# A two-layer graph attention network: the order in which the node tiles are walked

## The chip, the core and the metric

The kernel runs on one core of a Trainium2 chip. The core has five engines that run side by side: TensorE (PE in the profile, with its weight loads as PEld), VectorE (DVE), ScalarE (ACT), GpSimd (POOL) and SyncE (SP). POOL issues the indirect DMAs (gathers and scatters by a list of rows), SP most of the plain ones. Sixteen DMA engines move the data. The metric is the device time of one execution in microseconds, as the median of several runs.

## The reference, cut to what matters

There are 10,000 nodes with 768 numbers each, and 170,000 directed edges `src -> dst`, sorted by `dst`, among them a loop at every node. To these the network adds one more loop a node. Two graph attention layers follow, the first with 4 heads of 256, the second with one head of 768. Everything is in float32.

```python
def gat_conv(x, edge_index, W, a_src, a_dst, bias, heads, out_ch, concat):
    xl = (x @ W).reshape(n, heads, out_ch)
    alpha_src = jnp.einsum('nhc,hc->nh', xl, a_src)
    alpha_dst = jnp.einsum('nhc,hc->nh', xl, a_dst)
    e = jax.nn.leaky_relu(alpha_src[src] + alpha_dst[dst], 0.2)
    m = jax.ops.segment_max(e, dst, num_segments=n)
    e = jnp.exp(e - m[dst])
    s = jax.ops.segment_sum(e, dst, num_segments=n)
    alpha = e / (s[dst] + 1e-16)
    out = jax.ops.segment_sum(xl[src] * alpha[:, :, None], dst, num_segments=n)
    ...
h = relu(layer_norm(gat_conv(x, ..., W1, ...))) + (x @ Wr1 + br1)
h1 = h
h = layer_norm(gat_conv(h, ..., W2, ...)) + (h1 @ Wr2 + br2)
return _layernorm(x + h)
```

For each node the rows of its in-neighbours are weighted by a softmax over its in-edges and added up. How much work a node makes depends on its in-degree.

## The kernel before, in words

**Preparation.** While PE computes `x @ W1` for all nodes and writes the products with their attention terms to a table in DRAM (`table1`, rows of 1033 numbers), the other engines sort the nodes by in-degree, from many to few, and write for each node the list of its in-neighbours. The sorted nodes are cut into 79 tiles of 128. `slot_counts` gives each tile a number of slots, the most in-edges that a node in it may have: tile 0 has 41 slots, tiles 1 to 5 have 27, 26, 25, 24 and 24, then the number falls slowly to 20 at tile 16, 16 at tiles 44 to 50, 15 at 51 to 58, 14 at 59 to 64, 13 at 65 to 69, 12 at 70 to 72, 11 at 73 to 75, and 10, 9 and 8 at tiles 76, 77 and 78. There are 1377 slots in all. Slot k of a tile holds, for each of the 128 nodes, the row number of its k-th in-neighbour.

**The order.** `TURNS` (line 96) is the order in which both layers walk the tiles. Before, it takes every other tile from 78 down to 0 and then the others from 1 up to 77. `FIRST` (line 98) gives each tile the place of its first slot in this order. Lines 663 to 666 bring both lists into the order of `TURNS`, so that inside the layers `t` counts turns and `SLOTS[t]` is the count of the tile whose turn it is. If any node doesn't fit its tile's slots, a general path is taken instead; it isn't taken here.

**The ring.** Both layers read the table rows through a `Ring` (line 434): a buffer in SBUF of 28 rows of 128 partitions in layer 1 and 38 in layer 2. The slots follow each other in it in the order of `TURNS`, across tiles. Each gather (line 418, issued by POOL) brings one slot, that is one row for each of the 128 nodes. The gather for slot q + size is written behind the weighted sum that frees slot q. In layer 2 a tile's first slot holds the tile's own rows, which lie together in the table and come by a plain DMA of SP (line 445).

**Layer 1** (`ordered_layer1`, lines 668 to 812). In a turn, the logits of all slots of the tile are computed and turned into weights (`weights_of`, `logits`, `normalised`); this needs all of the tile's rows. The first one to four slots (`on_pe`) are summed on PE by diagonal matrices, the others on DVE (`weigh`, lines 504 and 508), three of four after ACT has scaled the row (`multiply`, line 497). The sum is normalised on DVE (lines 563 to 566), and the residual product is added (line 765). Its transposes go through PE, ACT copies them (line 575), SP stores them (line 777), and PE multiplies them by `W2`; ACT copies the product, and SP stores it as the tile's rows of `table2` (line 730). The normalising and products of a tile stand in the turn of the next one. The weights of the next tile are made during the present one where its slots and a lead of 3 fit the ring (line 795); tiles with more than 25 slots don't, and the one with 41 goes through `attend_parts` in parts.

**Layer 2** (`ordered_layer2`, lines 814 to 946) begins when all of `table2` is stored. Per tile there are the gathers of its slots but the first, a fetch of the tile's rows of `x` (an indirect DMA of POOL) and of the stored transposes (SP), the residual product on PE (`residual`), and weights as before. DVE sums the first 512 columns (`weigh`), PE the other 256 by diagonal matrices (lines 859 and 860). `norms` normalises twice in the turn of the next tile (line 884 adds the residual), and POOL scatters the result rows to the output (line 893).

Of the kernel before, what the change touches and what calls it, by code (L numbers as in the profile page):

```python
# [78 lines left out]
def gnn_kernel(ctx, tc, x, x_cols, src, dst, src_col, dst_col, W1, a_src1, a_dst1, b1, g1, be1, Wr1, br1,  # L79
# [9 lines left out]
    NT = -(-N // P)  # L89
# [3 lines left out]
    CAPS = slot_counts(N, n_edges)  # L93
    SLOTS = CAPS

    TURNS = list(range(NT - 1, -1, -2))
    TURNS += sorted(set(range(NT)) - set(TURNS))
    FIRST, TOTAL = [0] * NT, 0
    for t in TURNS:
        FIRST[t], TOTAL = TOTAL, TOTAL + SLOTS[t]  # L100
# [389 lines left out]
    def doubled(e, t):  # L490
        nc.vector.tensor_scalar(e[:, 0], e[:, 0], loops[:, TURNS[t]:TURNS[t] + 1], None, op0=OP.mult)

# [169 lines left out]

    SLOTS, FIRST = [SLOTS[t] for t in TURNS], [FIRST[t] for t in TURNS]

    def nodes(t):
        return order[:, TURNS[t]:TURNS[t] + 1]

    def ordered_layer1():
        nonlocal ps_big
        with tc.tile_pool(name="b1", bufs=1) as pool, tc.tile_pool(name="small1", bufs=2) as small, \  # L670
# [53 lines left out]
            def store(t):  # L724
# [4 lines left out]
                full = None  # L729
                nc.sync.dma_start(table2[TURNS[t] * P:(TURNS[t] + 1) * P, :], row)  # L730

# [485 lines left out]
```

## Time and profile before

| what | value |
| --- | --- |
| median of 3 runs | 5479.6 us (5479.25 to 5485.96) |
| profiled execution, own time | 5488.77 us |
| its span, first to last instruction | 5487.0 us |
| mean granted clock of TensorE | 0.938 |
| first and last store of `table2` (layer 1) | 975.0 and 3483.8 us |
| first gather of layer 2 | 3487.9 us |
| last gather, last scatter issued | 5425.8 and 5477.2 us |
| gathers, both layers | 2675, 969 ns each on POOL |
| DMA | 1581.74 MB, 288 GB/s over the span |

Times in the profile are counted from the first instruction. A busy share over the whole span mixes three stages: the preparation with the first product (to about 900 us), layer 1 and layer 2. In a timeline, "[0.30 <-issue]" after an instruction says how long its engine was idle before it and what ended that. The granted clock is the share of TensorE's clock pulses that were let through. The chain of work that ended last has only the last scatter in it here, so the order of work was read from the timelines.

### The profile page before, as it was taken

The numbers are of one execution on the slowest core, as the hardware profiler recorded it, in microseconds if no ns is written. First come the engines' busy times: TensorE is split into PE (matmuls) and PEld (weight loads), VectorE is DVE, ScalarE is ACT, GpSimd is POOL, SyncE is SP. The second block draws the span as 40 slices with busy tenths as digits, with TensorE's granted clock in tenths as the row PEclk, the third lists the DMA queues.
The fourth block names the chain that finished last, engine by engine and source line by source line (L and its number), as shares of the span: only waits on it lengthen the run. The fifth ranks groups of instructions, "written<-read, shape, count | busy, mean of one in ns | idle before, by whom it ended". The sixth has DMA issues, their size and how long they took to land. (4 is left out here: it accounts for less than half of the span.)

```text
span 5487.0 us, 58297 instructions
## 1 busy us (share of the span) xinstructions
PE 4754.0 (87%) x15032; PEld 2827.1 (52%) x15032; DVE 4328.8 (79%) x7766; ACT 3148.0 (57%) x8255; POOL 3247.4 (59%) x3238
## 2 busy tenths in 40 slices
PE   8999997999999875478999999799988746888998
PEld 3444443555555543245555555466655524555665
DVE  5784244899998888788999999498877786778998
ACT  3433344788888877678888888244433312333444
POOL 2445455455566555455665554377777775777774
PEclk9999998999999988789999999899998877899999
DMA  4333625899999988789999997699999987999996
GB/s 152 124 95 82 94 91 202 316 328 339 339 361 347 344 303 301 285 315 345 353 359 347 341 329 263 239 340 360 345 333 321 336 297 258 331 323 349 349 355 240
DMA packets 457866, 1581.74 MB, mean 288 GB/s; under 512 B 111851, under 2 KB 116011, under 8 KB 457526
## 3 DMA queue, kind: packets, MB, share of 16 engines
q0 software_dynamic: 328704, 1339.21, 68.3%
q1 hardware_dynamic: 126768, 235.29, 13.1%
q10 hardware_dynamic: 2054, 3.42, 0.2%
q8 instruction: 126, 2.06, 0.2%
q14 instruction: 214, 1.75, 0.1%
HBM read 1431.80 MB, written 146.23 MB: 288 GB/s over the span
## 5 line engine op out<-in xcount | busy, mean ns | idle before, releaser
L418 POOL DMA_INDIRECT ring<-table,slots x2675 | 2591.7, 969 | 1635.6 <-DVE acc L508 402.4
L508 DVE SCALAR_TENSOR_TENSOR acc<-ring,e,acc 128x256 f32<-128x256 f32 (+1 forms) x2538 | 1572.0, 619 | 127.5 <-PE acc L709 52.0
L497 ACT ACTIVATE ring<-ring,e 128x256 f32<-128x256 f32 x3320 | 1351.0, 505 | 0.0
L504 DVE TENSOR_TENSOR acc<-acc,ring 128x1024 f32<-128x1024 f32 x830 | 1022.5, 1232 | 72.8 <-ACT ring L497 1.2
L874 PE MATMUL big<-wr,w 128*128 128x512 f32 (+1 forms) x2528 | 857.9, 493 | 0.0
L169 PE MATMUL big<-w,xT 128*128 128x512 f32 x1896 | 827.7, 598 | 28.9 <-DMA w<-in_W_dram 11.2
L169 PE MATMUL big<-wr,xT 128*128 128x512 f32 x1896 | 834.1, 596 | 0.7 <-ACT xT L575 0.7
L169 PE MATMUL big<-w,hT 128*128 128x512 f32 (+1 forms) x2528 | 832.1, 486 | 1.2 <-ACT hT L575 1.2
L860 PE MATMUL big<-ring,diagonals 128*128 128x256 f32 x2672 | 660.8, 409 | 185.3 <-ACT diagonals L859 177.0
L860 PEld LDWEIGHTS big<-ring,diagonals 128*128 128x128 f32 x2672 | 543.6, 206 | 299.4 <-ACT diagonals L859 201.2
L169 PEld LDWEIGHTS big<-w,hT 128*128 128x128 f32 x2528 | 478.4, 189 | 375.0 <-issue 341.3
L709 PE MATMUL acc<-ring,diagonals 128*128 128x256 f32 x1816 | 456.6, 409 | 247.9 <-ACT diagonals L703 216.5
L874 PEld LDWEIGHTS big<-wr,w 128*128 128x128 f32 x2528 | 488.1, 193 | 350.3 <-issue 317.7
L169 PEld LDWEIGHTS big<-w,xT 128*128 128x128 f32 x1896 | 362.7, 192 | 491.9 <-issue 472.8
L169 PEld LDWEIGHTS big<-wr,xT 128*128 128x128 f32 x1896 | 356.9, 192 | 421.2 <-issue 420.3
L709 PEld LDWEIGHTS acc<-ring,diagonals 128*128 128x128 f32 x1816 | 370.1, 206 | 326.8 <-ACT diagonals L703 235.7
L859 ACT ACTIVATE diagonals<-ident,e 128x128 f32<-128x128 f32 x1336 | 399.6, 387 | 155.6 <-DVE e L488 117.9
L554 ACT ACTIVATE sd<-mv,eps 128x1 f32<-128x1 f32 x237 | 69.8, 294 | 614.0 <-DVE mv L552 613.6
L650 DVE TENSOR_TENSOR scr<-big,as_b 128x1024 f32<-128x1024 f32 x79 | 96.8, 1225 | 391.9 <-ACT row L647 391.9
L655 POOL TENSOR_TENSOR row<-row,none 128x1024 f32<-128x1024 f32 x79 | 187.2, 2369 | 280.5 <-ACT row L647 279.9
L703 ACT ACTIVATE diagonals<-ident,e 128x128 f32<-128x128 f32 x908 | 278.5, 387 | 96.4 <-DVE e L488 96.4
L475 ACT ACT_TABLE_LOAD x153 | 196.3, 1283 | 233.1 <-DVE e L474 205.9
(172 smaller groups left out, 3895.5 us busy)
## 6 DMA issues: line engine op xcount, KB each, us to landing
ring<-table,slots POOLq DMA_INDIRECT x2675, 6.5
table<-row SPq DMA_DIRECT2D x79, 516.0 KB, 3.6
h_d<-hT SPq DMA_DIRECT2D x79, 512.0 KB, 7.2
w<-h_d SPq DMA_DIRECT2D x79, 512.0 KB, 8.4
table<-row SPq DMA_DIRECT2D x79, 385.0 KB, 6.2
ring<-table SPq DMA_DIRECT2D x79, 385.0 KB, 6.5
xT<-in_x_cols_dram SPq DMA_DIRECT2D x79, 384.0 KB, 4.5
wr<-in_Wr_dram SPq DMA_DIRECT2D x2, 3072.0 KB
```

The costliest lines, as they stand in the source:

```text
L169: nc.tensor.matmul(p[:, c:e], aT[:, j, :], w[:, j, c:e], start=(j == 0), stop=(j == k - 1))
L418: nc.gpsimd.indirect_dma_start(out=to, out_offset=None, in_=table, in_offset=bass.IndirectOffsetOnAxis(ap=index, axis=0), **more)
L475: nc.scalar.activation(e, e, AF.Exp)
L497: nc.scalar.activation(row[:, s], row[:, s], AF.Copy, scale=e[:, h:h + 1])
L504: nc.vector.tensor_add(acc[:, :c], acc[:, :c], row[:, :c])
L508: nc.vector.scalar_tensor_tensor(acc[:, s], row[:, s], e[:, h:h + 1], (acc if first is None else first)[:, s], op0=OP.mult, op1=OP.add)
L655: nc.gpsimd.tensor_add(row[:, :C1], row[:, :C1], b1_b)
L703: nc.scalar.activation(diagonals[:, k * H1 + i, :], ident, AF.Copy, scale=e[:, k, i:i + 1])
L709: nc.tensor.matmul(acc[:, c:d], diagonals[:, k * H1 + i, :], ring.slot(FIRST[t] + k)[:, c:d], start=(k == 0 and c % BANK == 0), stop=(k == ...
L859: nc.scalar.activation(diagonals[:, k % G, :], ident, AF.Copy, scale=e[:, k, :])
L860: nc.tensor.matmul(to, diagonals[:, k % G, :], ring.slot(FIRST[t] + k)[:, ON_PE2:C2], start=False, stop=(k == n - 1), skip_group_check=True)
L874: nc.tensor.matmul(r[:, c:d], hT[:, j, :], wr2[:, j, c:d], start=False, stop=(j == K1 - 1 and (d < C2 or not whole(t))), skip_group_check= ...
```

## The change

The order `TURNS` is made differently, and nothing else. After the change it takes all tiles from 78 down to 48 one by one, then every other tile from 47 down to 1, and then the others, 0, 2, 4 and so on, up to 46. `FIRST`, the slots' places in the ring and the order in both layers follow from it. In slots, the order before is 8, 10, 11, 12, 12, 13, ... 24, 26, 41, 27, 25, ... 11, 11, 9; after it is 8, 9, 10, 11, 11, 11, 12, ... 25, 27, 41, 26, 24, ... 17, 16, 16.

```diff
     CAPS = slot_counts(N, n_edges)
     SLOTS = CAPS
 
-    TURNS = list(range(NT - 1, -1, -2))
+
+    TURNS = list(range(NT - 1, NT * 3 // 5, -1)) + list(range(NT * 3 // 5, -1, -2))
     TURNS += sorted(set(range(NT)) - set(TURNS))
     FIRST, TOTAL = [0] * NT, 0
     for t in TURNS:
         FIRST[t], TOTAL = TOTAL, TOTAL + SLOTS[t]
```

## The prediction

> **What bounds the kernel now.** I read the page first, then the stretches by engine, then the order of events on single queues. A tile is 128 nodes of similar in-degree; its "slots" are the rows that it gathers from the table. Tile 0 has 41 slots, tile 77 has 9 and tile 78 has 8. The page's costliest groups say which work grows with slots: gathers on POOL, and the weighted sums on DVE.
>
> ```profile
> PE 4754.0 (87%) x15032; PEld 2827.1 (52%) x15032; DVE 4328.8 (79%) x7766; ACT 3148.0 (57%) x8255; POOL 3247.4 (59%) x3238
> ...
> L418 POOL DMA_INDIRECT ring<-table,slots x2675 | 2591.7, 969 | 1635.6 <-DVE acc L508 402.4
> L508 DVE SCALAR_TENSOR_TENSOR acc<-ring,e,acc 128x256 f32<-128x256 f32 (+1 forms) x2538 | 1572.0, 619 | 127.5 <-PE acc L709 52.0
> ```
>
> No engine is full over the span, so I cut the span at tile boundaries and asked for busy times by stretch. The stretches are: layer 1 with 10 to 13 slots going up, with 15 and 16 slots going up, around the largest tile, the last small tiles; then layer 2 with 11 and 12 slots going up, with 16 slots going up, with 16 slots coming down, and its end. Columns: length, busy time of PE, its weight load, DVE, ACT and POOL, granted clock, DMA share, GB/s.
>
> ```profile
> 975.00:1100.70 125.70, 120.67 (x392) 67.94 (x391) 112.66 (x180) 102.25 (x241) 62.10 (x66) 1.00 0.88 303
> 1323.60:1408.80 85.20, 82.18 (x281) 49.32 (x280) 78.19 (x126) 71.37 (x177) 48.47 (x51) 1.00 0.94 346
> 2105.00:2339.20 234.20, 121.92 (x377) 73.18 (x376) 192.38 (x296) 159.59 (x406) 117.51 (x124) 0.75 0.83 291
> 3392.80:3468.20 75.40, 71.50 (x230) 39.64 (x229) 60.72 (x93) 49.08 (x115) 3.76 (x4) 1.00 0.31 114
> 3546.70:3613.40 66.70, 66.70 (x238) 44.17 (x237) 61.52 (x137) 29.59 (x70) 44.76 (x47) 1.00 0.91 306
> 3811.50:3877.40 65.90, 61.08 (x223) 41.08 (x222) 57.17 (x122) 27.83 (x67) 50.02 (x52) 1.00 0.97 352
> 5136.90:5200.10 63.20, 59.16 (x207) 38.82 (x206) 57.84 (x122) 27.55 (x66) 48.11 (x50) 0.97 0.97 358
> 5430.80:5487.00 56.20, 38.91 (x140) 25.78 (x139) 42.68 (x91) 16.07 (x35) 3.98 (x4) 0.89 0.15 54
> ```
>
> The reader is to see that layer 1's small tiles fill PE (120.67 of 125.70 us) while POOL is half idle, and that layer 1 closes with almost no gathers left (3.76 us of POOL in 75.40). In layer 2's middle POOL is busy 50.02 of 65.90 us, which looks like slack. The timeline of POOL shows that it isn't:
>
> ```profile
> 3564.86 0.97 POOL L418 DMA_INDIRECT ring<-table,slots  x1 [0.30 <-issue]
> 3569.03 0.94 POOL L418 DMA_INDIRECT ring<-table,slots  x1 [3.19 <-PE big L860]
> 3570.28 0.94 POOL L418 DMA_INDIRECT ring<-table,slots  x1 [0.30 <-DVE acc L508]
> ...
> 5424.52 0.94 POOL L418 DMA_INDIRECT ring<-table,slots  x1 [0.30 <-issue]
> 5425.77 1.11 POOL L418 DMA_INDIRECT ring<-table,slots  x1 [0.30 <-issue]
> ...
> 5441.03 1.02 POOL L893 DMA_INDIRECT out_dram<-out,order  x1 [10.30 <-ACT out L891]
> ```
>
> Every gather is followed by 0.30 us in which nothing can run, so 1.25 us is the least distance between two. In the stretch 5000 to 5425 no wait is above 0.3 us: the queue is full. Adding all gaps above 0.31 us from the first normalised tile (3546.7) to 5430.8 gives 85.6 us, 57 of them by the end of tile 0; 9.3 us lie in the first seven small tiles, where the ring of 38 rows is full and PE is slower than POOL (the 3.19 above). So layer 2 is the POOL queue: 1298 gathers, 79 residual fetches and 79 scatters.
>
> In layer 1 I use the stores of finished rows, one a tile:
>
> ```profile
> 1000.13 0.32 SPq L730 DMA_DIRECT2D table<-row  x1
> 1025.27 0.32 SPq L730 DMA_DIRECT2D table<-row  x1
> ...
> 3443.10 0.32 SPq L730 DMA_DIRECT2D table<-row  x1
> 3468.23 0.33 SPq L730 DMA_DIRECT2D table<-row  x1
> ...
> 3483.77 0.32 SPq L730 DMA_DIRECT2D table<-row  x1
> ```
>
>
> Up to 13 slots the stores come every 25.1 us, up and down alike; the last takes 15.5. Read the same way, 14 slots take 26.9 going up and 26.3 coming down, 15 and 16 take 28.3 (DVE has no idle there), 18 take 30.3, 20 about 35 up and 34 down. These are costs of a tile, not of its place.
>
> **The change part by part.** It permutes tiles; in layer 1 two tiles fewer straddle the ring's end (46 for 48), which saves two additions of 0.20 us on DVE and two copies on ACT, and nothing else is added or removed. A moved tile takes all of its work along: in layer 1 its gathers and x fetch on POOL, its two stores on SP, its sums, products and copies; in layer 2 one gather fewer (its own rows come through SP), the fetch, the scatter, and SP's load of h. The list preparation copies the same columns to other offsets, beside the layer-0 products: nothing. The fifteen odd tiles 49 to 77 (200 slots) move from each layer's end to its front half, between their neighbours; 2 to 46 and 1 to 47 swap sides. Both layers still open with tile 78; both now close on tile 46 with 16 slots.
>
> *Layer 1, start.* The second tile has 9 slots, not 10. DVE waited 0.57 us at 937.5 for that tile's last rows; one gather less removes it: −0.6.
>
> *Layer 1, small tiles.* Eight tiles of 9 to 12 slots follow on each other going up, at PE's 25.1: 201. Before, four of them took 101.0 going up (starts of the line that adds the residual, L765, 948.5 to 1049.5) and 71, 73 and 75 took 72.5 at the end, where DVE ran ahead of PE; tile 77 stood last and is counted next. 201 less 25.1 for tile 77 is 176, against 173.5: +2.5. Three tiles of 14 slots pay 26.9 instead of 26.3 to 26.5: +1.2.
>
> *Layer 1, end.* Tile 77's 25.1 comes into the row and a tile of 28.3 goes out of it: −3.2. Closing then costs, from L765 of tile 44: 1.1, then 13 rows on DVE at 20.0 (tile 47's own row of sums, 3042.88 to 3065.60, less 2.7 for the next tile's logits, of which there is none), 4.4 of normalising; then 18.1 to the last store, which is today's 23.2 without the 5.1 that the finished row waited for PE. Sum 43.7; today 3441.4 to 3483.8 is 42.4: +1.3. Layer 1 in all: +1.2.
>
> *The largest tiles.* Before, 26 → 41 → 27 come in the order 24, 26, 41, 27, 25; after, 25, 27, 41, 26, 24. A tile gets its weights ahead only if its slots + 3 fit the ring of 28, so three tiles per layer still go without (27, 41, 26). I take 0. Bounds: the unprepared 26 took 42.1 going up, the 27 took 52.6 coming down; half of that 10 either way, ±5 a layer.
>
> *Layer 2, POOL's count.* From its first gather (3487.9) to its last (5425.8) POOL issues 1449 of 1456; seven come behind, two fetches and five scatters. With 38 rows of ring and 16 slots a tile, the last gather goes out at row 10 of tile 42: all fetches are gone by then (that of tile 46 at row 8), and so is the scatter of tile 40: three scatters stay behind. Four more ahead of the last gather, each (1937.9 − 91.6 idle) / 1449 = 1.274: +5.1. The 91.6 is 85.6 and some 6 of DMA waits at the start.
>
> *Layer 2, going up.* With a full ring a tile takes what PE needs: 15.5 for 10 slots, 16.0 for 11, 17.6 for 12, 18.0 for 13 (distances of L884); 9 slots, by the slope of the first two, 15.1. POOL needs slots + 1 instructions of 1.274. The difference is lost: 2.4, 1.5, 0.7, 1.0 and 0.2. Over all fourteen it is 10.1, over the six of them that went up before 4.7: +5.4. Bounds: 0, if POOL's own slower instructions fill it, and +11, if the measured 9.3 of seven tiles counts in full for twice as many.
>
> *Layer 2, end.* Today 61.2 us pass from the last gather to the end (5487.0). After, POOL is the bound until its last gather, and the state is that of tile 47 coming down: its last gather at 5156.2, L884 of the tile two before it at 5158.9, 2.7 later. Then tile 44 at its own work, 19.6 (PE and DVE have 59.16 and 57.84 us for three such); tile 46 without a successor's product, like tile 77's 10.7 plus seven rows of 0.76 = 16.0; then today's 14.1. Sum 52.4: −8.8. Bounds: −1.9, if it keeps the steady lag of 45.2 from last gather to L884 (45.2 + 14.1 = 59.3), and −12.
>
> Layer 2: 5.1 + 5.4 − 8.8 = +1.7. Both layers: **+2.9 us**. The profiled execution took 5488.8 (span 5487.0 and 1.8 around it), 0.17% above the median 5479.6; 5488.8 + 2.9 = 5491.7 on its scale, and on the median's **5482.5**.
>
> A rule that speaks against the new end: in the stretch of 16 slots coming down the granted clock is 0.97, around the largest tile 0.75, because PE waits for rows there; among the small tiles it is 1.00. The Trainium skill, "TensorE: Matmul & The Clock Gate", section "HAM oscillation — how this bites in real kernels", says that a pause of PE over some 3.4 us puts its clock to half. By the rule two such pauses at layer 2's new end would cost about 1.7 us each, an estimate from that page: 5486 instead of 5482.5. I stay with the rows, since the 19.6 already is a stretch with that clock.
>
> **The rivals.**
> (a) *POOL runs dry on the long climb of layer 2 (slower).* Thirty tiles with small steps come first, and what POOL loses behind a full ring is not caught up. The first seven tiles lose 1.33 us each. If all 29 between tile 78 and tile 48 lose that, it is 38.6 instead of 9.3: +29 in place of +5.4, so 5506. It decides from about 0.8 us a tile (23 us, so +14 in place of +5.4, and +11 in all). For it: 14 slots pace 18.5 on PE, close to POOL's 19.1. Against it: from tile 62 on the loss is 0.0.
> (b) *Gathers bound layer 1 as well, and shorter ends are kept (faster).* From the last gather of a tile to its L765 pass 62.9 us at tile 77, 53.3 at tile 47: −9.6. With −8.8 in layer 2, +5.1, and nothing lost on the climb: −13.3, 5466. Against it: POOL in layer 1 waits for DVE and PE in each tile (62.10 busy of 125.70).
> (c) *The order at the peak matters*: if an unprepared 27 on the way up costs what it cost coming down, and the 26 gains nothing, +10.5 in layer 1 and +13.2 in layer 2 (37.4 against 24.2): 5506. The opposite would be as large. Against it: what one loses, its neighbour gains.
>
> **How the numbers follow.** A measurement here can tell 0.2%, 11 us. Forecast (within 11 us): 0.68. (a) 0.14, (b) 0.11, (c) 0.07, of which 0.05 slower. So faster 0.13, same 0.68, slower 0.19. With every bound on one side, peak included, the terms give −16 to +25 (5464 to 5505). All of them together is unlikely; I begin at 5467, beside (b), and end at 5497, which holds the upper bounds of the climb and of the end together (5495). What lies above, (a) and (c) at 5506, is some one in ten, and less lies below.
>
> **What would show it.** Stores of layer 1 25.1 us apart until the tiles of 14 slots, the last one some 1 us later; POOL in layer 2 without gaps from the tiles of 14 slots on, idle 12 to 18 us before them; three scatters behind the last gather and some 52 us to the end; around tile 0 the same sum. Wrong would be: gaps of 1 us a tile among 14 and 15 slots (a), a shorter layer 1 (b), or stretches at the peak that differ by over 10 us (c).

## The result and the profile after

The changed kernel takes 5497.67 us in the median (eleven runs, 5491.32 to 5502.47), the kernel before 5481.47 us beside it (eleven runs, 5471.83 to 5486.93). The ratio is 1.0028, with a 95% interval of 1.0019 to 1.0038: slower by 0.28%, or 16.2 us. The profiled execution took 5498.19 us with a span of 5496.4 us.

The page of the changed kernel first (busy time, share of the span and instructions of each engine, and the group of all gathers):

```profile
span 5496.4 us, 58267 instructions
...
PE 4756.6 (87%) x15032; PEld 2828.9 (51%) x15032; DVE 4330.7 (79%) x7764; ACT 3148.4 (57%) x8253; POOL 3248.6 (59%) x3238
...
L419 POOL DMA_INDIRECT ring<-table,slots x2675 | 2591.1, 969 | 1654.5 <-DVE acc L509 430.2
```

The work is the same to within 3 us on every engine. What has grown is the idle time of POOL ahead of its gathers, from 1635.6 to 1654.5 us over both layers. So the time isn't in any operation; it is in when POOL may issue.

Next the stretches by engine, from the kernel before. They are layer 1 from its first to its last store; layer 2 from its first to its last gather; in it the tiles of up to 13 slots going up; the eight tiles of 23 slots and more; and from the last gather to the end. Columns: length, busy time of PE, its weight load, DVE, ACT and POOL with counts, granted clock, DMA share, GB/s.

```profile
975.00:3483.80 2508.80, 2187.40 (x7226) 1304.77 (x7224) 2189.03 (x3381) 2021.03 (x4993) 1363.10 (x1406) 0.95 0.90 323
3487.87:5425.77 1937.90, 1620.67 (x5545) 1090.00 (x5546) 1568.18 (x3231) 720.94 (x1769) 1406.34 (x1449) 0.91 0.93 333
3546.69:3649.52 102.83, 102.83 (x366) 68.11 (x365) 95.19 (x213) 46.58 (x109) 71.36 (x75) 1.00 0.93 325
4362.74:4691.98 329.24, 190.91 (x653) 131.83 (x652) 234.49 (x430) 84.43 (x221) 221.94 (x222) 0.78 0.84 288
5425.77:5487.00 61.23, 43.94 (x161) 29.59 (x159) 47.43 (x103) 19.86 (x42) 8.03 (x8) 0.90 0.21 75
```

The same stretches of the changed kernel:

```profile
967.70:3477.40 2509.70, 2188.30 (x7227) 1304.93 (x7225) 2192.99 (x3384) 2021.67 (x4992) 1362.65 (x1407) 0.95 0.89 323
...
3481.40:5443.30 1961.90, 1647.09 (x5632) 1108.11 (x5633) 1576.23 (x3255) 728.54 (x1783) 1412.07 (x1452) 0.91 0.92 330
3541.01:3766.26 225.25, 225.25 (x796) 148.40 (x795) 206.63 (x463) 102.02 (x234) 157.89 (x162) 1.00 0.92 330
4639.22:4974.12 334.90, 193.57 (x650) 133.68 (x649) 234.55 (x431) 84.48 (x221) 222.42 (x223) 0.78 0.83 284
5443.30:5496.40 53.10, 20.31 (x74) 13.31 (x72) 39.79 (x79) 12.11 (x27) 3.94 (x4) 0.74 0.12 42
```

Layer 1 is the same: 2508.80 us from store to store before, 2509.70 after. Layer 2 from its first gather to the end went from 1937.90 + 61.23 = 1999.1 us to 1961.90 + 53.10 = 2015.0 us: +15.9, which is the difference of the medians. (The spans differ by only 9.4, mainly because the work ahead of layer 1, whose code is the same in both, took 905.0 us in the one execution and 899.9 in the other.) In the row of the tiles of up to 13 slots PE is busy in all of the 225.25 us, 796 matmuls of it without a pause. The eight largest tiles, the same eight in both, take 334.90 for 329.24.

To divide the 15.9 I went through POOL's timeline of layer 2 and added up, region by region, what lies between two of its instructions beyond the usual 0.30 us. What is left, divided by the number of instructions, is their spacing. The last column is the pair of kernels of experiment 5, with the same orders in layer 2.

| term of layer 2, us | forecast | before to after | experiment 5 |
| --- | --- | --- | --- |
| four more instructions ahead of the last gather (1449, 1453) | +5.1 | +5.1 | +5.1 |
| idle, tiles of up to 13 slots going up | +5.4 | 8.9 to 18.0: +9.1 | 8.8 to 16.7: +7.9 |
| idle, tiles of 23 slots and more | 0 | 39.7 to 44.8: +5.1 | 27.9 to 35.4: +7.5 |
| idle, tiles of 17 to 22 slots coming down | 0 | 16.7 to 18.9: +2.2 | 15.7 to 19.1: +3.4 |
| idle, all the rest | 0 | +0.3 | +0.6 |
| spacing without idle (1.2761 to 1.2776; 1.2789 to 1.2786) | 0 | +2.2 | −0.4 |
| from the last gather to the end | −8.8 | 61.2 to 53.1: −8.1 | 61.6 to 53.0: −8.6 |
| sum | +1.7 | +15.9 | +15.5 |

### The profile page after: what moved, and what is told of

Same layout as the page of the kernel before. It is cut to its first block, busy times and chain, and to the rows that moved or that the text cites. A ratio compares the mean times of both kernels' runs of the same rounds, so it can differ in the third digit from the quotient of the medians.

```text
span 5496.4 us, 58267 instructions
## 1 busy us (share of the span) xinstructions
PE 4756.6 (87%) x15032; PEld 2828.9 (51%) x15032; DVE 4330.7 (79%) x7764; ACT 3148.4 (57%) x8253; POOL 3248.6 (59%) x3238
## 5 line engine op out<-in xcount | busy, mean ns | idle before, releaser
L419 POOL DMA_INDIRECT ring<-table,slots x2675 | 2591.1, 969 | 1654.5 <-DVE acc L509 430.2
L654 ACT ACTIVATE scr<-scr 128x256 f32<-128x256 f32 x632 | 253.6, 402 | 123.2 <-DVE scr L651 123.2
```

The source lines that it names most:

```text
L419: nc.gpsimd.indirect_dma_start(out=to, out_offset=None, in_=table, in_offset=bass.IndirectOffsetOnAxis(ap=index, axis=0), **more)
L654: nc.scalar.activation(m[:, s], m[:, s], AF.Copy, accum_out=row[:, C1 + i * H1 + h:C1 + i * H1 + h + 1])
```

## The experiments

The orders of the two layers are separated by letting layer 2 have its own list of turns (`before_order()` and `after_order()` make the two lists; the cut below is from the kernel in which layer 2 alone is changed). The ring of layer 2 then reads the columns of the lists through a table, and the stored transposes are kept by tile, not by turn. All kernels of experiments 2 to 5 have this edit:

```diff
-    TURNS = list(range(NT - 1, -1, -2))
-    TURNS += sorted(set(range(NT)) - set(TURNS))
+    TURNS, TURNS2 = before_order(), after_order()
...
+    COLUMNS2 = [FIRST[t] + k for t in TURNS2 for k in range(SLOTS[t])]
...
-                    gather(self.slot(q), self.table[:, :], slots[:, q:q + 1])
+                    c = self.columns[q]
+                    gather(self.slot(q), self.table[:, :], slots[:, c:c + 1])
...
-                    nc.sync.dma_start(h1_d[t - 1], hT.rearrange("p k n -> p (k n)"))
+                    nc.sync.dma_start(h1_d[TURNS[t - 1]], hT.rearrange("p k n -> p (k n)"))
...
-                nc.sync.dma_start(hT, h1_d[t])
+                nc.sync.dma_start(hT, h1_d[TURNS[t]])
...
         ordered_layer1()
+        TURNS, FIRST, SLOTS = TURNS2, FIRST2, SLOTS2
```

In experiments 2 to 4 the kernel before itself took 5791 to 5828 us on the chips that they ran on. By the kernels with the old layer 2 that were traced there, some 300 of the extra 310 us on one chip and 335 of 345 on the other are in layer 2. Each kernel is compared with the kernel before on its own chip, and what that means for the theory is said under experiment 2.

### 1. The changed kernel again, beside experiment 5

> The changed kernel as it is, where the kernel before takes some 5790 us and TensorE pauses in layer 2. If the two layers' changes add up: layer 1 +10 to +13 us, layer 2 -6 to -9 us, together +1 to +7 us. If the loss of the judged runs has nothing to do with which queue bounds layer 2: +16 us here too.

Measured: 5499.49 us against 5483.30, ratio 1.0024 (1.0013 to 1.0035), +16.2 us as before. Layer 1 from store to store takes 2505.4, layer 2 from first to last gather 1965.4 and then 52.5. The parts of POOL's idle time agree with the first trace to 1.5 us (tiles up to 13 slots 16.6 for 18.0, tiles from 23 slots 44.3 for 44.8), and the spacing is 1.2804 for 1.2776. So the parts of idle time belong to the order, and the spacing changes from one execution to the next by more than the +2.2 in the table (0.0028 us an instruction are 4 us): that term is not the order's. The chip was one on which the kernel before takes 5483 us, so what was expected of a chip with 5790 us wasn't put to the test.

### 2. One layer's order at a time

Layer 1 new and layer 2 old (`TURNS, TURNS2 = after_order(), before_order()`), on two chips:

> Layer 1 walks the tiles in the new order, layer 2 in the old one. Theory (the loss is POOL's queue in layer 2): no change, within 3 us of before; from layer 1's first gather to layer 2's first gather 2582 us, as in both profiles (2582.9 before, 2581.5 after). Rival (layer 1 pays too, its small tiles or its end on 16 slots): +5 to +16 us. Second rival (the new order of columns in the list of neighbours matters by itself): +16 us here, since that list follows layer 1's order.

> The kernel with the new order in layer 1 alone, again, because the first time the kernel before itself took 5791 us, 5.7% more than in the runs that the prediction was judged by, all of it in layer 2, whose rows landed late; POOL's queue wasn't the bound there. If the kernel before takes some 5481 us now: theory, within 3 us of before (layer 1 neutral); rival, +10 us, as in the first try (2601.9 us from layer 1's first gather to layer 2's first, against 2589 to 2593 with the old order).

Layer 1 old and layer 2 new, in three comparisons:

> Layer 1 in the old order, layer 2 in the new one. Theory: the whole loss, +13 to +19 us against before; POOL's idle time between layer 2's first and last gather 104 to 110 us (90.1 before, 106.8 after), 18 of it in the 13 tiles with at most 13 slots that go up, and 53 us from the last gather to the end. Rival (layer 1 pays): 0 to +8 us.

> The new order in layer 2 alone, again. If the kernel before takes some 5481 us: theory, +13 to +19 us, POOL idle 104 to 110 us between layer 2's first and last gather. Where layer 2 waits for rows again (before at 5791 us): -6 us, as in the first try, since POOL's queue isn't the bound.

> The new order in layer 2 alone, third try, for a chip on which the kernel before takes some 5481 us and POOL's queue bounds layer 2. There: theory, +13 to +19 us, with POOL idle for 104 to 110 us between layer 2's first and last gather (90.1 before) and 53 us from the last gather to the end. Rival (layer 1 carries part of the loss): 0 to +8 us. On a chip like the two of the tries before, where TensorE pauses in layer 2: -6 us again.

Measured:

| kernel | us | kernel before beside it | ratio (95%) |
| --- | --- | --- | --- |
| layer 1 new | 5796.95 | 5791.24 | 1.0018 (1.0006 to 1.0031) |
| layer 1 new, again | 5843.67 | 5828.26 | 1.0022 (1.0007 to 1.0037) |
| layer 2 new | 5785.65 | 5791.24 | 0.9990 (0.9979 to 1.0000) |
| layer 2 new, again | 5821.22 | 5828.26 | 0.9985 (0.9972 to 0.9998) |
| layer 2 new, a third time | 5782.67 | 5792.63 | 0.9988 (0.9975 to 1.0001) |

That is the opposite of what the traces of before and after say. But these chips run layer 2 in another way. The windows of layer 2, from 3 us behind its first gather to its last: the kernel with layer 1 new, whose layer 2 is the old one,

```profile
3505.10:5739.30 2234.20, 1745.85 (x5539) 1136.56 (x5540) 1574.00 (x3234) 735.78 (x1773) 1398.75 (x1447) 0.86 0.84 288
```

and the kernel with layer 2 new, from 0.7 us behind the first gather:

```profile
3497.00:5732.00 2235.00, 1743.86 (x5583) 1142.24 (x5584) 1582.40 (x3260) 739.42 (x1783) 1412.92 (x1452) 0.86 0.84 290
```

From first to last gather they take 2237 and 2236 us where 1938 and 1962 were seen above; POOL has nearly the same busy time as there, and 394 and 379 us of idle time for 90 and 107. The timeline of PE in the second kernel shows where much of it comes from (an entry in square brackets is the idle time just before, and what ended it):

```profile
4014.06 3.96 PE L887 MATMUL big<-ring,diagonals 128*128 128x256 f32 x17
4019.75 0.38 PE L887 MATMUL big<-ring,diagonals 128*128 128x256 f32 x1 [1.73 <-issue]
4021.85 4.40 PE L887 MATMUL big<-ring,diagonals 128*128 128x256 f32 x12 [1.72 <-issue]
```

PE stops in the middle of a row of matmuls, here for 1.7 us at a time, and the trace names nothing that it waits for. Its waits from 3560 to 5470 us (engine, tile and line, what it waited for: total, times, longest) are led by these:

```profile
PE big L887 <- issue: 239.8, 129, 22.4
...
PE big L901 <- issue: 39.0, 29, 2.4
```

In the same stretch of the kernel before, in the first trace, no such wait is listed; the largest sum is

```profile
PE big L860 <- ACT diagonals L859: 177.0, 29, 22.7
```

PE is also busy for longer, 1745.85 and 1743.86 us where 1620.67 and 1647.09 were seen, at a granted clock of 0.86 for 0.91. So here POOL waits for what PE has to free, and an order can't be charged with what it does to POOL. One thing is open in this reading: the traces of these chips hold no landing times of the gathers (the others do, 6.5 us in the median), so some of the waits that they put down to nothing may be for a DMA. Between these two traces the new layer 2 gains 15.4 us of idle time and 11.8 at the end, and loses 14 by count and spacing: −13. These runs say nothing on why the change lost its 16 us. They do show that the sign of an order depends on the bound, and that the new layer 1 costs something here (first gather of layer 1 to first gather of layer 2: 2601.9 us against 2589 to 2595 in the kernels with the old order of the first chip; 2608.3 against 2596 to 2599 on the second). On the chips without the pauses no such difference is to be seen: 2581.5 and 2578.3 with the new order, 2582.9, 2574.8 and 2578.1 with the old.

### 3. The other parity

Layer 2 goes up over the even tiles and ends on tile 47, so that 26 goes up alone, as before, and tiles of 25 and 27 come down:

```diff
+        o = list(range(NT - 1, NT * 3 // 5, -1)) + list(range(NT * 3 // 5 - 1, -1, -2))
+        return o + sorted(set(range(NT)) - set(o))
```

> Layer 2 alone in a third order: 78 down to 48 one by one, then 46, 44 ... 2, 0, and 1, 3 ... 47. The climb and the end are the changed kernel's, the largest tiles come in the old order (24, 26, 41, 27, 25 slots). If the 5 us more idle time of POOL around the largest tile belong to their order: POOL idle 101 to 103 us, +9 to +12 us against before. If they are chance: like the layer 2 of the changed kernel, +13 to +19 us. If the end on a medium tile is what costs: +16 us.

Measured: 5785.77 us against 5791.24, ratio 0.9990 (0.9980 to 1.0000), the same as layer 2 new on this chip; POOL's idle time at the tiles of 23 slots and more is 88.5 us against 85.5. On a chip where PE pauses the parity makes no difference. Whether it does where POOL is the bound was not tried.

### 4. Small tiles between the large ones

Layer 2 opens with 47, 45 and so on, a small tile stands behind each of the 31 largest, and it ends on 44 and 46:

```diff
...
+        small = list(range(NT - 1, m - 1, -1))
+        spots = sorted(o[1:-2], key=lambda t: t)[:len(small)]
+        after = dict(zip(spots, small))
+        return [u for t in o for u in ([t, after[t]] if t in after else [t])]
```

> Layer 2 alone in an order without a climb of small tiles: it opens with 47, 45, 43 ... (16 and 17 slots), goes up to tile 0 and down again, with a small tile (48 to 78) behind each of the larger ones, and closes on 44 and 46 like the changed kernel. Theory (what POOL loses behind a full ring is the cost, and the end on medium tiles is a gain of some 8 us less 5 us of count): no loss on the climb, POOL idle 50 to 85 us in place of 90.1, 53 us of end, so 8 to 43 us faster than before. Rival (an end on medium tiles costs, whatever stands ahead): +10 to +16 us. Second rival (a large tile behind a small one waits longer for its rows, since the ring has 38): 20 us or more slower.

> Layer 2 without the climb of small tiles, large and small ones in turn, end on 16 slots, again. If the kernel before takes some 5481 us: theory, 8 to 43 us faster than before, POOL idle 50 to 85 us; rival (the end on medium tiles costs): +10 to +16 us. Where layer 2 waits for rows: +10 us, as in the first try.

> Large and small tiles in turn in layer 2, end on 16 slots, third try. On a chip where the kernel before takes some 5481 us: theory, 8 to 43 us faster than before, POOL idle for 50 to 85 us; rival (the end on medium tiles costs): +10 to +16 us. On a chip like the two before: 0 to +10 us again.

Measured: 5801.67 against 5791.24, ratio 1.0021 (1.0009 to 1.0033); 5825.59 against 5828.26, 0.9999 (0.9986 to 1.0012); 5810.50 against 5792.63, 1.0036 (1.0022 to 1.0049). In the first of them POOL's idle time at the tiles of 23 slots and more falls to 33.4 us from 89.8 with the old layer 2. But the total is 406.8 against 394.2: at the tiles of up to 16 slots, most of which stand between larger ones now, it goes from 98.9 to 197.1. So most of the idle time has moved from the large tiles to their small neighbours. Slower twice and no difference once; it is no improvement there, and on a chip without the pauses, for which the gain was expected, it didn't run.

### 5. Less PE work in layer 2, with both orders

To see whether PE's load is what holds POOL up, layer 2 leaves out the residual product for every tile of more than 13 slots. Layer 1 keeps the old order in both kernels; they differ only in the order of layer 2.

```diff
-                    nc.tensor.matmul(r[:, c:d], ident, xt[:, c:d], start=True, stop=False,
-                                     skip_group_check=True)
-                    for j in range(K1):
+                    light = SLOTS[t] > 13
+                    nc.tensor.matmul(r[:, c:d], ident, xt[:, c:d], start=True,
+                                     stop=light and (d < C2 or not whole(t)), skip_group_check=True)
+                    for j in range(0 if light else K1):
```

> Old order in both layers; layer 2 leaves out the residual product of h1 for all tiles of more than 13 slots (65 of 79; the x that is added to it stays), so that PE has some 10.7 us a tile less there and POOL's queue should be the bound again, as in the judged runs, while the 14 small tiles keep PE's floor. Theory: layer 2 falls back to POOL's count, 1449 instructions of 1.275 and 95 to 125 us of idle time before the last gather, some 2000 to 2035 us for the whole layer in place of 2290 to 2330. If the rows' DMA were what holds layer 2 up here, it stays above 2200.

> The same product left out, layer 2 in the new order, layer 1 in the old one. Theory: with POOL as the bound the climb of 13 small tiles loses some 40 to 46 us against some 25 for the old order's six, 4 more instructions are ahead of the last gather (+5), the end is 8 to 12 us shorter: +8 to +18 us against the same kernel with the old order. Rival (order makes no difference to what POOL loses; only the end counts): -6 to -12 us against it.

Measured: 5466.95 us with the old order in layer 2, ratio 0.9973 (0.9962 to 0.9983) to the kernel before; 5481.63 us with the new one, 0.9998 (0.9989 to 1.0007). The new order costs 14.7 us here (14.8 ± 4.5 by the means and the spread of the runs). The windows of the old order (layer 2's gathers; tiles of 23 slots and more; the end):

```profile
3474.24:5399.86 1925.62, 1044.69 (x3464) 749.78 (x3465) 1566.64 (x3231) 720.58 (x1769) 1410.03 (x1448) 0.74 0.94 335
...
4346.65:4665.22 318.57, 110.08 (x396) 85.00 (x395) 234.15 (x430) 84.44 (x221) 223.20 (x222) 0.66 0.87 297
5399.86:5461.50 61.64, 44.36 (x162) 29.78 (x160) 47.43 (x103) 19.91 (x42) 7.95 (x8) 0.88 0.21 75
```

and of the new one:

```profile
3479.34:5429.10 1949.76, 1071.99 (x3586) 768.88 (x3586) 1575.30 (x3255) 728.83 (x1783) 1413.54 (x1452) 0.74 0.93 332
...
4634.61:4961.29 326.68, 111.58 (x399) 86.06 (x398) 234.22 (x430) 84.50 (x221) 223.58 (x223) 0.65 0.85 291
5429.10:5482.10 53.00, 12.01 (x40) 8.68 (x38) 39.74 (x79) 12.12 (x27) 3.94 (x4) 0.62 0.12 44
```

Three things follow. First, PE loses 1620.67 − 1044.69 = 576 us of work between the first and the last gather, and the stretch gets shorter by 12.3 us only: here layer 2 is POOL's queue. (What was expected of layer 2's length, 2000 to 2035 us in place of 2290 to 2330, had the chips of experiments 2 to 4 in mind. This chip has none of their pauses, and its layer 2 took 1987 us, where the kernel before in the first trace took 1999.) That the sixteen DMA engines set the pace instead, with a mean busy share of 0.94 here, doesn't fit: the gathers of layer 1 bring rows a third longer (1033 numbers for 770) and still take 0.97 us each on POOL with at least 0.30 us behind them, as those of layer 2 do; and a queue that goes on at this pace without a wait, as in the forecast's stretch from 5000 to 5425 us, isn't held up by rows that land late. Second, the loss is layer 2's order and nothing else, since layer 1 is identical in the two kernels: it comes out at the same size as that of the whole change. Third, the extra idle time at the largest tiles, +7.5 us, is there although PE is busy for only a third of that stretch, so it isn't the residual product of PE that makes it. The sum came as expected, +8 to +18 us, but its parts were smaller: the climb lost 8.8 and 16.7 us where some 25 and 40 to 46 were expected, and POOL's idle time with the old order was 74 us, not 95 to 125.

## What the prediction had right and wrong, step by step

The forecast was 5482.5 us and no measurable change, that is less than 11 us either way; "slower" had a chance of 0.19. Measured were 5497.67 us, 16.2 more than before. That lies at the upper end of the range, 5467 to 5497 (the kernel before took 1.9 us more beside it than on record), and it is partly luck that the range reached so far: its end held 5.6 us more for the climb and 6.9 for the end of layer 2, of which 3.7 and 0.7 came; the rest of the time is in places that the sum had at nothing. Layer 1's +1.2 came out as +0.9, layer 2's +1.7 as +15.9. Two steps were off: the size of the floor that PE sets for small tiles, and the largest tiles, taken at 0.

**What bounds.** Right. Layer 2 is POOL's queue on chips where the kernel before takes some 5481 us (experiment 5), and layer 1 is not.

**Layer 1, +1.2.** Right in sum. Stores are 25.1 us apart for most of the tiles of up to 13 slots (26.0 to 27.5 for the last three), and the last comes 0.9 us later after the first than before. The timeline of SP, changed kernel:

```profile
992.90 0.32 SPq L731 DMA_DIRECT2D table<-row  x1
1018.03 0.32 SPq L731 DMA_DIRECT2D table<-row  x1
...
3457.79 0.33 SPq L731 DMA_DIRECT2D table<-row  x1
3477.41 0.32 SPq L731 DMA_DIRECT2D table<-row  x1
```

A tile costs there about what it costs in any place. By parts the sum owes something to chance: the last store comes 19.6 us after the one ahead of it, for 15.5 before, and that is made up by the tiles of 17 slots and more, which take 5.3 us less by the distances of the stores (1603.9 to 1598.6) and which the forecast had at nothing. Nor can these traces tell 1 us: the two kernels of experiment 5, whose layer 1 is the same, need 2501.8 and 2505.0 us for it. Rival (b), gathers that bound layer 1 as well, fell.

**POOL's count, +5.1.** Right: 1453 instructions for 1449 up to the last gather.

**Layer 2's end, −8.8.** Right: −8.1 and −8.6. POOL's timeline shows three scatters behind the last gather, as forecast, and 53.1 us to the end where 52.4 was forecast:

```profile
5443.33 0.95 POOL L419 DMA_INDIRECT ring<-table,slots  x1 [0.30 <-PE big L861]
5453.09 1.01 POOL L894 DMA_INDIRECT out_dram<-out,order  x1 [8.81 <-ACT out L892]
5472.18 1.00 POOL L894 DMA_INDIRECT out_dram<-out,order  x1 [18.08 <-ACT out L892]
5486.73 0.98 POOL L894 DMA_INDIRECT out_dram<-out,order  x1 [13.56 <-POOLq L1166]
```

The rule on the clock that the forecast set against the new end had nothing to act on. The Trainium skill, "TensorE: Matmul & The Clock Gate", section "HAM oscillation — how this bites in real kernels", has a pause of PE of more than some 3.4 us put its clock to half. Behind the last gather PE pauses once while it still has work, for 1.22 us, and its granted clock is 1.00 until its last matmul ends at 5464.83. The 0.74 of the whole stretch comes from the 31.57 us behind that, at 0.57, in which PE has nothing left to do (before, 1.00 up to 5473.0 and 0.54 behind it). So none of the 3.4 us that the forecast's estimate from that page made of it was to be paid.

**Layer 2 going up, +5.4.** The place and the mechanism were right, the size was not: +9.1, and +7.9 in experiment 5. POOL runs far ahead of the small tiles, fills the ring, and waits once a tile. Its waits in the changed kernel, from 10 slots on:

```profile
3562.93 0.97 POOL L419 DMA_INDIRECT ring<-table,slots  x1 [3.74 <-DVE acc L509]
3579.67 0.95 POOL L419 DMA_INDIRECT ring<-table,slots  x1 [2.47 <-DVE acc L509]
3596.85 0.95 POOL L419 DMA_INDIRECT ring<-table,slots  x1 [2.09 <-DVE acc L509]
...
3631.21 0.95 POOL L419 DMA_INDIRECT ring<-table,slots  x1 [2.11 <-DVE acc L509]
```

The mis-sized number is the floor that PE sets for a tile. I took it from the distances of L884, an instruction of DVE: 15.5 us for 10 slots, 16.0 for 11. In the first tiles of the kernel before these marks lay closer together than PE's work, as they do when DVE is still catching up. PE's own starts give the floor. In the kernel before the diagonal matmuls of the two tiles in question begin 16.74 us apart:

```profile
3551.31 4.58 PE L860 MATMUL big<-ring,diagonals 128*128 128x256 f32 x20
...
3568.05 5.01 PE L860 MATMUL big<-ring,diagonals 128*128 128x256 f32 x22
```

and after the change, with 11 slots, 17.18 us apart, with nothing between them left empty:

```profile
3578.70 5.01 PE L861 MATMUL big<-ring,diagonals 128*128 128x256 f32 x22
3583.56 1.02 PE L872 MATMUL big<-w,ident 128*128 128x512 f32 x2
3584.41 7.03 PE L875 MATMUL big<-wr,w 128*128 128x512 f32 x16
3591.28 0.59 PE L872 MATMUL big<-w,ident 128*128 128x256 f32 x2
3591.71 3.62 PE L875 MATMUL big<-wr,w 128*128 128x256 f32 x16
3595.26 0.69 PE L856 MATMUL big<-b,ones 1*128 1x256 f32 x2
3595.88 5.01 PE L861 MATMUL big<-ring,diagonals 128*128 128x256 f32 x22
```

Those lines were in the trace of before; read there, with 0.44 us a slot, the floors for 9 to 13 slots are 16.3, 16.7, 17.2, 17.6 and 18.0. POOL needs slots + 1 instructions of 1.276. It loses 3.5, 2.7, 1.9, 1.0 and 0.2 us a tile: 15.8 over the thirteen tiles, 7.0 over the six of before, +8.8, where +9.1 and +7.9 were measured. PE's starts in the changed kernel bear the floors out: 16.32, 16.75, 17.18, 17.61 and 18.04 us apart for 9 to 13 slots.

**Rival (a).** Its mechanism is this same one; its price wasn't paid. It needed 0.8 us a tile on the whole climb, and from 14 slots on nearly nothing is lost: 0.9 us over 19 tiles, 0.05 each, as the forecast said.

**The largest tiles, 0.** This step failed. I argued that what one tile loses its neighbour gains, and took 0 with ±5; measured were +5.1 and +7.5 us of POOL's idle time, and 334.90 for 329.24 us in the stretch. I also said that three tiles a layer go without weights made ahead (27, 41, 26). That holds for layer 1 with its ring of 28 rows. In layer 2 the ring has 38, and 26 or 27 slots and a lead of 3 fit it: only tile 0 and the tile behind it go without, 27 before and 26 after. All of the +5.1, and 5.5 of the +7.5, are on the way up to tile 0. The waits of POOL there over 1 us, in the kernel before, with 24 and 26 slots ahead of tile 0:

```profile
4398.78 0.94 POOL L418 DMA_INDIRECT ring<-table,slots  x1 [1.58 <-PE big L871]
4420.74 0.94 POOL L418 DMA_INDIRECT ring<-table,slots  x1 [2.14 <-DVE acc L508]
4436.83 0.94 POOL L418 DMA_INDIRECT ring<-table,slots  x1 [5.14 <-PE big L860]
```

and after, with 24, 25 and 27 slots:

```profile
4675.50 0.95 POOL L419 DMA_INDIRECT ring<-table,slots  x1 [1.57 <-PE big L861]
4697.38 0.95 POOL L419 DMA_INDIRECT ring<-table,slots  x1 [3.30 <-DVE acc L509]
4713.17 0.94 POOL L419 DMA_INDIRECT ring<-table,slots  x1 [2.83 <-PE big L861]
4737.46 0.95 POOL L419 DMA_INDIRECT ring<-table,slots  x1 [1.97 <-DVE acc L509]
4753.89 0.94 POOL L419 DMA_INDIRECT ring<-table,slots  x1 [6.61 <-PE big L861]
```

By the tiles of more than 22 slots, idle time is 8.1 us going up before and 14.8 after (+6.7), 19.7 and 18.6 in tile 0 itself, 11.9 and 11.5 coming down. The old order goes up over 23, 24, 26 and the new one over 23, 24, 25, 27: one such tile more.

What holds up the rows is to be seen on DVE. In the turn of the 25-slot tile, in the changed kernel, it computes the logits of 14 of the next tile's 27 rows and then waits for the other 13, without which the weights can't be made; in this time it sums nothing and so frees no row of the ring:

```profile
4725.32 0.18 DVE L468 TENSOR_TENSOR e<-ring,ad 128x14 f32<-128x14 f32 x1
4735.22 0.17 DVE L468 TENSOR_TENSOR e<-ring,ad 128x13 f32<-128x13 f32 x1 [9.71 <-DMA ring<-table,slots]
```

On the way up DVE's waits at this line, all but one (6.7) ended by a DMA's landing as the trace has it, are 4.9, 6.5 and 9.0 us before, for the rows of the tiles of 23, 24 and 26 slots, and 5.4, 6.7, 9.7 and 9.7 after, for those of 23, 24, 25 and 27. POOL's waits of 3.30 and 1.97 above end with DVE's first sum behind the last two of them, that of 2.14 before in the same way. This accounts for those three; the others, the 5.14 and 6.61 above all, end with PE's matmuls and aren't explained by it.

How much such a tile costs is not settled. One more pair of neighbours (24 and 25) on the way up together exceeds the ring's 38 rows by more than 10, and I read the rise as some 4 to 6 us for it. But on the way down the new order has one such pair fewer (26 and 24, for 27 and 25, 25 and 24), and idle time there is 11.9 and 11.5 us, in experiment 5 11.3 and 12.6: no fall to match. The order with the other parity, which could tell, was measured only on a chip where PE pauses. Experiment 5 rules out PE's residual product as the cause of the rise. So the largest tiles belonged in the sum as a rise, not as 0; what makes its size stays open.

**Rival (c)**, the order at the peak, had this place. Its price came from an unprepared 27 going up costing the 37.4 us that it cost coming down. But in layer 2 it is the tile behind tile 0 that goes unprepared, so the 27 going up took 25.0 us and the 26 behind tile 0 took 37.0: the two tiles changed roles, and there the price is nearly nothing. The cost is in the waits on the way up instead.

**The small rest.** Tiles of 17 to 22 slots coming down lose 2.2 and 3.4 us more, which the forecast didn't have; why, I don't know. Spacing added 2.2 in the first pair and −0.4 in the second, so it is no effect of the order. That the sum of the terms comes so close to the 16.2 of the medians is chance to that extent.

In all, of the 14.2 us that layer 2's sum was short, 3.7 are the floor of the small tiles, 5.1 the largest tiles, 2.2 the tiles coming down, 2.2 spacing, 0.7 the end and 0.3 the rest.

## What to carry to other kernels

Where one queue bounds a stage, an order of work is judged by adding up that queue's idle time region by region: a gain at one end (−8 us here) is easily outweighed by gaps of 2 to 4 us in places that seem only to have been rearranged. Read the pace of a stage from the starts of the engine that sets it, not from the marks of one that follows it, because a follower that is catching up shows intervals that are too short. "What one tile loses its neighbour gains" didn't hold here: with a full ring, POOL's waits weren't made up. And a condition in the code (does the next tile fit the ring?) has to be worked out for each ring that it is used with.

## What was not expected of the hardware

Layer 2's PE is busy for 1620.67 of 1937.90 us, 84%, and yet 576 us of its work can be taken out for 12 us of time; POOL, busy for 1406.34 us, 73%, is the bound, because each indirect DMA of 0.95 us is followed by at least 0.30 us in which it issues nothing.

The same kernel before took 5481 to 5483 us on some chips and 5791 to 5828 us on others, nearly all of the difference in layer 2, where PE pauses, often for 1.7 us at a time, with nothing in the trace to release it. Under these pauses the layer 2 that loses 15 to 16 us elsewhere gains 6 to 10, and the new layer 1, neutral elsewhere, costs 6 to 15. Where the pauses come from stays open, and so does the reason for the new layer 1's cost under them.
